# The causal mask of an attention layer: one product on the whole array, or four on parts of it

## Chip, core and metric

The kernel runs on one core of a Trainium2 chip. The metric is the device time of one execution in microseconds (us). The engines of the core run side by side, each through its own list of instructions: TensorE (matrix products; PE in the profile, its weight loads PEld), VectorE (DVE), ScalarE (ACT), GpSimd (POOL) and SyncE (SP, which issues DMAs). SBUF is the core's memory and PSUM is where TensorE writes; both have 128 partitions.

## What is computed

Two transformer layers on 4 sequences of 512 tokens of 256 features: layer 0 is causal attention with 16 heads of 16 features and a mixture of experts, layer 1 is attention and a gated network with 4-bit weights. The change is in layer 0's attention:

```python
x = x + _L0_attn_ref(_layernorm(x, axis=-1), L0_attn_w_project, L0_attn_w_out)
# in _L0_attn_ref:
qkv = jnp.einsum('bsd,od->bso', x, w_project)      # q, k, v of 16 heads
att = jnp.einsum('bhqd,bhkd->bhqk', q, k) / math.sqrt(HEAD_DIM)
causal = jnp.triu(jnp.ones((s, s), dtype=bool), k=1)
att = jnp.where(causal[None, None, :, :], jnp.float32(-1000000000.0), att)
att = jax.nn.softmax(att, axis=-1)
out = jnp.einsum('bhqk,bhkd->bhqd', att, v)
```

## The kernel before

Tokens are handled in blocks of 128. `j` (0 to 3) is the block of queries, `s` the sequence, `g` a group of four heads; the four heads of a group lie on the four quarters of the partitions, 32 each (16 features and helper rows). A batch is one `(j, s)` with 4 groups in block 0, 2 in block 1 and 1 in blocks 2 and 3. That makes 4 + 8 + 16 + 16 = 44 batches. `nk = (j + 1) * 128` is the number of keys, `nb` the number of groups of the batch.

For each batch the following steps are made:

- `greatest(n)` (line 679) computes the scores of queries by keys, one product for each head and group: 32 rows of the array, since a head has 32 partitions. The four heads go to four PSUM tiles, one bank each, from the pool `l0_sc` of five.
- `mask(n)` (line 694) adds the causal mask to the last 128 keys of each group: a product of an identity matrix `ident_h` (bf16) with `later` (bf16, 0 where the key is not later than the query, -1e30 elsewhere), added to the scores in PSUM. There is one product for each of the four heads; it repeats `later` for the `nb` groups. Then VectorE takes the largest score of each query (line 706).
- `shift(n)` (line 711) turns these maxima (line 716) and four DMAs of SP write them into a helper row of the queries (line 721).
- `powers(n)` (line 728) computes the scores a second time, keys by queries, with the maxima subtracted by the helper rows (line 738). ScalarE takes the exponential (line 747) and GpSimd clears what is later than the query (line 757).
- `mixed(n)` (line 765) multiplies by the values (line 774), on 32 columns of the array for each head, and ScalarE copies the result (line 782). `divided` (line 786) divides by the sum and projects.

The constants are made on GpSimd at the start, lines 498 to 511: a fill of `qk` with -1, a fill with 0, the copy `ident_h`, the fill and the select of `later`. Behind them on GpSimd stand the two powers of the first normalisation (line 653), then the fills of `blanks` (lines 520 to 522), the power of line 182, the fills of line 491 and `split_biases`.

What sets the order is a plan that the program works out when it is built: TensorE, VectorE, ScalarE and GpSimd take their instructions in the order in which they are written, and SP does up to batch 3; later a scheduler places SP's DMAs. In the loop over batches (line 886), `greatest(n + 1)`, `mask(n + 1)` and `shift(n + 1)` come first, then `fill` gives a budget of TensorE and VectorE costs to streams of other work, then `mixed(n - 1)` and `powers(n)`, then a second `fill`. The streams are generators that yield an engine, a cost, a gap and a condition: projections of the next block, the logits of the experts (`lg_ps`) and their results (`eo`) by `dense` (line 249), their routing on VectorE (lines 386 to 441), and the sums. So behind a mask, TensorE finds products of these streams as a rule.

```python
        for n in range(NBT):
...
                    greatest(n + 1)
...
                    mask(n + 1)
                    shift(n + 1)
...
            fill(PE=(2.0, 2.0, 1.8, 1.6)[j], DVE=2.6)
...
                    mixed(n - 1)
                powers(n)
```

Of the kernel before, what the change touches and what calls it, by code (L numbers as in the profile page):

```python
# [9 lines left out]
BF16 = mybir.dt.bfloat16  # L10
I32 = mybir.dt.int32
AF = mybir.ActivationFunctionType
ALU = mybir.AluOpType
# [3 lines left out]
P = 128  # L17
# [6 lines left out]
NEG = -1.0e30  # L24
# [8 lines left out]
def tile_transformer(  # L33
# [18 lines left out]
    nc = tc.nc  # L52
# [23 lines left out]
    ident = const.tile([P, P], F32, name="ident")  # L76
# [9 lines left out]
    mask32 = const.tile([P, 32], F32, name="mask32")  # L86
# [377 lines left out]
    with ExitStack() as l0:  # L464
        w0 = l0.enter_context(tc.tile_pool(name="w_l0", bufs=1))
# [19 lines left out]
        def blank(j, i):  # L485
# [15 lines left out]
        )  # L501
        nc.gpsimd.memset(qk[:, :, NBLK].rearrange("p g s q -> p g (s q)"), 0.0)

        ident_h = w0.tile([P, P], BF16, name="ident_h")
        nc.gpsimd.tensor_copy(ident_h, ident)
        later = w0.tile([P, P], BF16, name="later")
        nc.gpsimd.memset(later, 0.0)
        nc.gpsimd.affine_select(
            out=later, in_=later, compare_op=ALU.is_ge, fill=NEG,
            base=0, pattern=[[-1, P]], channel_multiplier=1,  # L510
        )
        bs = b1.tile([P, 2, 512], F32, tag="hi4", name="bs")
        rows = b1.tile([P, 12, P], BF16, tag="part", name="rows")
        sel = rows[:, :8]
# [161 lines left out]
        def queries(j, g):  # L676
            return qk[:, g, 4 + j % 2]

        def greatest(n):

            j, s, gs = batches[n]
            nk = (j + 1) * P
            tiles = [ps_sc.tile([P, 512], F32, tag="sc", name=f"s1_{n}_{h}") for h in range(4)]
            for b, g in enumerate(gs):
                for h in range(4):
                    r = slice(32 * h, 32 * h + 32)
                    nc.tensor.matmul(  # L687
                        tiles[h][:, b * nk : (b + 1) * nk].rearrange("p (c k) -> p c k", k=P),
                        lhsT=queries(j, g)[r, s], rhs=qk[r, g, : j + 1, s, :],
                        start=b == 0, stop=False,  # L690
                    )
            open_scores[n] = tiles

        def mask(n):

            j, s, gs = batches[n]
            nk, nb = (j + 1) * P, len(gs)
            tiles = open_scores.pop(n)
            for ps in tiles:
                nc.tensor.matmul(  # L700
                    ps[:, : nb * nk].rearrange("p (b k) -> p b k", b=nb)[:, :, j * P :],
                    lhsT=ident_h, rhs=later.unsqueeze(1).to_broadcast([P, nb, P]),
                    start=False, stop=True,
                )
            for h, ps in enumerate(tiles):
                nc.vector.tensor_reduce(  # L706
                    maxes[:, :nb, h],
                    ps[:, : nb * nk].rearrange("p (b k) -> p b k", b=nb), AX.X, ALU.max,
                )
# [126 lines left out]
        ps = ps_mm.tile([P, 4, P], F32, tag="mm", name="idle")  # L836
        for i in range(5):
            nc.tensor.matmul(
                ps, lhsT=ident, rhs=ident.unsqueeze(1).to_broadcast([P, 4, P]),
                start=not i, stop=i == 4,  # L840
# [33 lines left out]
        for piece in inputs_T(1, second[0], xT):  # L874
            pass
        greatest(0)
        mask(0)
        shift(0)
        inputs = {1: Stream(projections(1, xT))}
# [6 lines left out]
        for n in range(NBT):  # L886
            j, s, gs = batches[n]
# [7 lines left out]
            with tc.high_priority(offset=AHEAD):  # L895
                if n + 1 < NBT:
                    greatest(n + 1)
                if n + 1 < NBT:
                    mask(n + 1)
                    shift(n + 1)  # L900
# [76 lines left out]
    with ExitStack() as l1:  # L977
# [3 lines left out]
        for kv, i in [(slice(None), slice(HPK + 1, HPK + 2))] + [  # L981
            (slice(kv, kv + 1), slice(0, HPK + 1)) for kv in range(NKV)
        ]:
            for hc in range(2):
                tc.keep_in_program_order(
                    nc.sync.dma_start(
                        out=wqkv[:, hc, kv, i], in_=w_qkv[hc * P : (hc + 1) * P, kv, i]
# [239 lines left out]
        for p in range(-1, NP):  # L1227
            j, kv = divmod(p, NKV)
# [59 lines left out]
    with ExitStack() as f1:  # L1288
# [186 lines left out]
        f, k = firsts  # L1475
# [3 lines left out]
        for i in range(NBLK * NJ):  # L1479
            j, jj = divmod(i, NJ)  # L1480
# [160 lines left out]
```

## Time and profile before

| what | value |
|---|---|
| median of 3 runs | 1139.03 us (1138.77 to 1139.43) |
| profiled execution, its own time | 1140.53 us |
| its span, first to last instruction | 1138.8 us |
| granted TensorE clock, mean | 0.999 |
| ScalarE, GpSimd busy | 509.5 us (45%), 247.2 us (22%) |
| mask, line 700: loads, products | 176, 176; from 24.0 to 354.5 us |
| product of 128, 256, 512 columns: mean length | 222, 275, 382 ns (128, 32 and 16 times) |
| weight load of the mask: mean length | 97 ns |

The profile is of one execution. Lengths of products reach from the first column entering to the last result written, so that successive products overlap: the distance from start to start tells what a product costs, and its length does not. A product in f32 stands as two passes. "128\*128" is the number of rows and columns of the array that an instruction uses; "32\*128" uses a quarter of the rows, and four such products on four quarters run side by side. The chain of work that ended last is followed back from the end, from each instruction to what released it. Time on an engine counts for the end only where this chain runs through it.

### The profile page before, as it was taken

The numbers are of one execution on the slowest core, as the hardware profiler recorded it, in microseconds if no ns is written. First come the engines' busy times: TensorE is split into PE (matmuls) and PEld (weight loads), VectorE is DVE, ScalarE is ACT, GpSimd is POOL, SyncE is SP. The second block draws the span as 40 slices with busy tenths as digits, with TensorE's granted clock in tenths as the row PEclk, the third lists the DMA queues.
The fourth block names the chain that finished last, engine by engine and source line by source line (L and its number), as shares of the span: only waits on it lengthen the run. The fifth ranks groups of instructions, "written<-read, shape, count | busy, mean of one in ns | idle before, by whom it ended". The sixth has DMA issues, their size and how long they took to land.

```text
span 1138.8 us, 19760 instructions
## 1 busy us (share of the span) xinstructions
PE 1109.8 (97%) x7430; PEld 711.7 (62%) x7430; DVE 842.3 (74%) x1856; ACT 509.5 (45%) x1190; POOL 247.2 (22%) x319
## 2 busy tenths in 40 slices
PE   9999999999999999999999999999999999999998
PEld 5666555555555445555555556556787788888885
DVE  6675988999999962867873695577479877778665
ACT  1445545665556543444444353243324444444442
POOL 8322222221111000000000000000064444353433
PEclk9999999999999999999999999999999999999999
DMA  4450010000000500000000002242002002002000
GB/s 133 110 134 5 17 25 2 2 1 3 2 2 2 184 2 1 1 1 1 1 1 1 1 2 37 66 110 68 18 1 54 22 19 75 1 19 75 18 2 19
DMA packets 32287, 35.13 MB, mean 31 GB/s; under 512 B 6024, under 2 KB 23176, under 8 KB 32192
## 3 DMA queue, kind: packets, MB, share of 16 engines
q1 hardware_dynamic: 31376, 32.69, 11.0%
q10 hardware_dynamic: 816, 1.18, 0.4%
q8 instruction: 59, 0.97, 0.3%
q14 instruction: 36, 0.29, 0.1%
HBM read 23.17 MB, written 6.29 MB: 26 GB/s over the span
## 4 chain that ended last, share of the span: by engine, by line
PE 67%; DVE 23%; ACT 4%; issue 3%; POOL 1%; DMA 1%; SPq 1%; DVEq 0%; POOLq 0%; ACTq 0%
PE qk_ps L1037 10%; PE lg_ps L249 8%; PE o L1128 8%; PE eg L963 7%; PE eo L249 7%; PE gu_first L963 5%; DVE mx L706 3%; PE yx L1344 3%; PE s L738 3%; PE s L687 3%; PE av L774 2%; PE yy L1344 2%; DVE it L1420 2%; DVE th L1419 2%; PE qk_ps L555 2%
## 5 line engine op out<-in xcount | busy, mean ns | idle before, releaser
L1037 PE MATMUL qk_ps<-xT,wqkv 128*128 128x512 f32 x320 | 148.7, 599 | 3.5 <-ACT v L1023 1.7
L249 PE MATMUL lg_ps<-rw,xT 128*128 128x512 f32 x256 | 122.5, 601 | 1.6 <-ACT aT L812 0.4
L249 PE MATMUL eo<-ew,xT 128*128 128x512 f32 x256 | 121.5, 600 | 1.1 <-ACT lg L312 0.5
L706 DVE TENSOR_REDUCE mx<-s 128x1 f32<-128x384 f32 (+3 forms) x176 | 100.5, 633 | 26.8 <-PE s L700 26.8
L1128 PE MATMUL o<-wpj,oT 128*128 128x256 f32 x512 | 119.1, 382 | 0.0
L757 POOL TENSOR_SCALAR_AFFINE_SELECT pt<-pt 128x256 f32<-128x256 f32 (+2 forms) x88 | 62.5, 715 | 243.3 <-ACT pt L747 242.5
L1128 PEld LDWEIGHTS o<-wpj,oT 128*128 128x128 f32 x512 | 96.0, 190 | 27.0 <-issue 13.5
L1037 PEld LDWEIGHTS qk_ps<-xT,wqkv 128*128 128x128 f32 x320 | 59.1, 190 | 73.2 <-issue 58.4
L747 ACT ACTIVATE pt<-s 128x512 f32<-128x512 f32 (+1 forms) x176 | 84.0, 563 | 37.6 <-PE s L738 37.6
L182 POOL TENSOR_TENSOR ln_rs<-rs_v,minus_half 128x4 f32<-128x4 f32 x12 | 13.6, 1135 | 366.0 <-DVE rs_v L181 366.0
L338 ACT ACTIVATE part<-eo,c 128x256 f32<-128x256 f32 x128 | 53.6, 472 | 84.0 <-PE eo L249 72.7
L1531 ACT COPY gu_first<-eg 128x512 f32<-128x512 f32 x28 | 16.0, 570 | 134.2 <-PE eg L963 129.9
L249 PEld LDWEIGHTS eo<-ew,xT 128*128 128x128 f32 x256 | 46.2, 190 | 46.3 <-issue 38.5
L249 PEld LDWEIGHTS lg_ps<-rw,xT 128*128 128x128 f32 x256 | 46.1, 190 | 46.3 <-issue 37.5
L1322 POOL TENSOR_TENSOR it<-it 128x512 f32<-128x512 f32 x30 | 38.2, 1273 | 146.6 <-PE gu_first L963 66.9
L312 ACT COPY lg<-lg_ps 128x512 f32<-128x512 f32 x64 | 37.6, 588 | 71.8 <-PE lg_ps L249 71.8
L1041 ACT COPY qT<-qk_ps 128x512 f32<-128x512 f32 x64 | 37.5, 586 | 64.7 <-PE qk_ps L1037 64.7
L1344 PE MATMUL yx<-it,wd 128*128 128x256 f32 x240 | 66.2, 379 | 0.0
L738 PE MATMUL s<-qk 32*128 32x128 f32 x1280 | 56.6, 287 | 0.7
L687 PE MATMUL s<-qk 32*128 32x128 f32 (+3 forms) x512 | 56.7, 465 | 0.4
L438 DVE SCALAR_TENSOR_TENSOR junk<-lg,w 128x256 bf16<-128x256 f32 x128 | 54.9, 429 | 0.0
L365 DVE TENSOR_TENSOR part<-part 128x512 f32<-128x512 f32 x32 | 22.4, 700 | 43.9 <-ACT part L338 43.9
(305 smaller groups left out, 2202.5 us busy)
## 6 DMA issues: line engine op xcount, KB each, us to landing
qk<-stage SPq DMA_DIRECT2D x56, 64.0 KB
wqkv<-in_w_qkv SPq DMA_DIRECT2D x8, 320.0 KB
rw<-in_router_w SPq DMA_DIRECT2D x8, 256.0 KB
ew<-in_expert_w SPq DMA_DIRECT2D x8, 256.0 KB
qk<-mT SPq DMA_DIRECT2D x128, 0.5 KB
wpj<-in_w_proj SPq DMA_DIRECT2D x1, 2048.0 KB
dq_sgu<-in_gate_up_s SPq DMA_DIRECT2D x64, 32.0 KB
xres<-in_x SPq DMA_DIRECT2D x3, 512.0 KB
```

The lines of the kernel that those rows point to most:

```text
L249: nc.tensor.matmul(ps, lhsT=xT[:, hc, (g % 4) * P : (g % 4 + 1) * P], rhs=w[:, hc, 2 * pair : 2 * pair + 2, :].rearrange("p e o -> p (e o) ...
L338: nc.scalar.mul(part[:, e % 4], ps[:, i], c[:, e : e + 1])
L438: stt(junk, d[:, e], 0.0, w1, ALU.is_gt, ALU.mult, accum_out=c1[:, e : e + 1])
L687: nc.tensor.matmul(tiles[h][:, b * nk : (b + 1) * nk].rearrange("p (c k) -> p c k", k=P), lhsT=queries(j, g)[r, s], rhs=qk[r, g, : j + 1, ...
L706: nc.vector.tensor_reduce(maxes[:, :nb, h], ps[:, : nb * nk].rearrange("p (b k) -> p b k", b=nb), AX.X, ALU.max,)
L738: nc.tensor.matmul(tiles[h][:, at : at + P], lhsT=qk[r, g, c, s, :], rhs=queries(j, g)[r, s], start=True, stop=True,)
L747: nc.scalar.activation(pt[:, i, : nb * nk], tiles[2 * pair + i][:, : nb * nk], AF.Exp, scale=0.25)
L757: nc.gpsimd.affine_select(out=last, in_=last, compare_op=ALU.is_ge, fill=0.0, base=0, pattern=pattern, channel_multiplier=-1,)
L963: nc.tensor.matmul(ps[:, w], lhsT=lhs(w), rhs=rhs, start=start and not i and not w, stop=i == len(terms) - 1 and w == 1, skip_group_check= ...
L1037: nc.tensor.matmul(ps, lhsT=wqkv[:, hc, kv, h, :], rhs=xT[:, hc, :], start=hc == 0, stop=hc == 1,)
L1128: nc.tensor.matmul(ys[t // 2][:, t % 2], lhsT=state["o"][:, h, t * P : (t + 1) * P], rhs=wpj[:, HPK * kv + h, :], start=kv == 0 and h == 0 ...
L1344: nc.tensor.matmul(ps, lhsT=lhs(jj), rhs=its[8 * j + jj][:, plane], start=start and not n, stop=n == 1, skip_group_check=not start,)
```

## The change

The identity becomes `pick`, 32 x 32 identities on each of the four quarters of the partitions (a copy of `mask32`, which VectorE has made from `ident` by then). `later` is selected quarter by quarter, so that each quarter holds the mask of its own 32 queries against keys counted from the quarter's own first. In `mask`, each head has four products in place of one, one for each 32 queries `c`. A product takes 32 rows of the array (those of the head's quarter) and 32 columns (those of the queries), and writes only the keys from `32 * c` on: 128, 96, 64 and 32 keys per group. The order is by `c`, then by head. The scores' own products now carry the flag `stop`, and the mask products skip a check of groups when the program is built.

```diff
-        ident_h = w0.tile([P, P], BF16, name="ident_h")
-        nc.gpsimd.tensor_copy(ident_h, ident)
+        pick = w0.tile([P, 32], BF16, name="pick")
+        nc.gpsimd.tensor_copy(pick, mask32)
         later = w0.tile([P, P], BF16, name="later")
         nc.gpsimd.memset(later, 0.0)
-        nc.gpsimd.affine_select(
-            out=later, in_=later, compare_op=ALU.is_ge, fill=NEG,
-            base=0, pattern=[[-1, P]], channel_multiplier=1,
-        )
+        for i in range(4):
+            r = slice(32 * i, 32 * i + 32)
+            nc.gpsimd.affine_select(
+                out=later[r], in_=later[r],
+                compare_op=ALU.is_ge, fill=NEG, base=0, pattern=[[-1, P]], channel_multiplier=1,
+            )
...
-                        start=b == 0, stop=False,
+                        start=b == 0, stop=b == len(gs) - 1,
...
-            for ps in tiles:
-                nc.tensor.matmul(
-                    ps[:, : nb * nk].rearrange("p (b k) -> p b k", b=nb)[:, :, j * P :],
-                    lhsT=ident_h, rhs=later.unsqueeze(1).to_broadcast([P, nb, P]),
-                    start=False, stop=True,
-                )
+            for c in range(4):
+                for h, ps in enumerate(tiles):
+                    r = slice(32 * h, 32 * h + 32)
+                    left_of = P - 32 * c
+                    nc.tensor.matmul(
+                        ps[32 * c : 32 * c + 32, : nb * nk].rearrange(
+                            "p (b k) -> p b k", b=nb
+                        )[:, :, j * P + 32 * c :],
+                        lhsT=pick[r],
+                        rhs=later[r, :left_of].unsqueeze(1).to_broadcast([32, nb, left_of]),
+                        start=False, stop=True, skip_group_check=True,
+                    )
```

## The prediction

> **What bounds the kernel now.** I read the page first, for who is busy and what the chain of work that ended last is made of:
>
> ```profile
> PE 1109.8 (97%) x7430; PEld 711.7 (62%) x7430; DVE 842.3 (74%) x1856; ACT 509.5 (45%) x1190; POOL 247.2 (22%) x319
> ...
> PE 67%; DVE 23%; ACT 4%; issue 3%; POOL 1%; DMA 1%; SPq 1%; DVEq 0%; POOLq 0%; ACTq 0%
> ```
>
> The second line is the chain by engine: TensorE sets most of the end and VectorE a quarter of it, so time on TensorE counts only where the chain runs through TensorE. The mask products stand in line 700, all 176 of them between 24 and 355 us. So I read the timeline of TensorE around one batch of block j = 2:
>
> ```profile
> 150.64 0.93 PE L687 MATMUL s<-qk 32*128 32x384 f32 x8
> 151.50 0.40 PE L700 MATMUL s<-later,ident_h 128*128 128x128 bf16 x4
> 151.74 1.94 PE L249 MATMUL eo<-ew,xT 128*128 128x512 f32 x4
> 153.60 0.86 PE L774 MATMUL av<-pt,va 128*32 128x128 f32 x24
> 154.40 1.58 PE L738 MATMUL s<-qk 32*128 32x128 f32 x24
> 156.33 0.70 PE L249 MATMUL eo<-ew,xT 128*128 128x512 f32 x1 [0.35 <-DVE xres L831]
> ```
>
> Columns: start, length, line, rows*columns of the array, shape, count. The four mask products start 0.06 us apart ((0.40 - 0.219)/3, where 219 ns is the median length in the table of line 700), and 0.24 us after their start the next work is there. So the mask is cheap already: 0.24 us of a batch of 7.6 us.
>
> Two more things stand in these lines. First, a change of shape costs a pause. The mask starts 0.86 us after L687, whose products stream only 2 x 0.32 us (384 columns, two passes, and L249's 512 columns take 0.43 us a pass) behind a first load of 0.11 us: 0.11 us over. L774 streams six groups of 0.109 us from 153.60, that is until 154.28 to 154.30, and L738 starts at 154.40. The same mask followed by another shape shows it alone:
>
> ```profile
> 182.19 0.40 PE L700 MATMUL s<-later,ident_h 128*128 128x128 bf16 x4
> 182.51 0.86 PE L774 MATMUL av<-pt,va 128*32 128x128 f32 x24
> ```
>
> 0.33 us to the next work here (182.18 by the load) against 0.24 above: **94 ns for the change of shape**. Second, a load that nothing covers. L249's first product lasts 648 ns behind the mask, 697 ns behind a wait (156.33) and 592 ns otherwise: its weights cost 105 ns when they are loaded after a pause, 56 ns when they were loaded during the mask.
>
> Last, the chain in order of time, for which mask products stand on it:
>
> ```profile
> 27.56 0.97 PE s L700 x4
> ...
> 55.23 0.54 PE s L700 x4
> ...
> 122.14 0.33 PE s L700 x4
> ...
> 145.01 0.18 PE s L700
> ```
>
> "x4" means that the chain passes through the mask to the next product: 1 of 4 batches in block 0 (512 columns), 6 of 8 in block 1 (256), 13 of 32 in blocks 2 and 3 (128). A single one means that it leaves through the first mask product to VectorE's maximum: 2 times in block 0, 5 times in blocks 2 and 3. In the others VectorE is last, and the mask is covered.
>
> **The change part by part.** In the built order of the changed program each batch has 16 loads and 16 products of 32 x 32 in place of 4 and 4; everything else on TensorE, VectorE and ScalarE stands in the same order. The columns streamed are 128, 96, 64 and 32 per head and group, in place of 128.
>
> *What 16 small products take.* No row shows 32*32. The nearest is L774, also narrow in columns:
>
> ```profile
> 153.60 0.32 PE L774 MATMUL av<-pt,va 128*32 128x128 f32 x4
> ```
>
> Four of 297 ns within 0.32 us: 7 ns from start to start. The bounds: 7 ns for all 16, and 60 ns, the pitch of the present mask. I take 10 ns, near the closer row, since four tiles are shown and sixteen are not. The load of 32 columns adds 25 ns (297 against 272 in L774's table).
>
> *Blocks 2 and 3.* Before: 238 ns to the next product and 56 ns of its load uncovered, 294 ns. After: 15 x 10 ns, 25 ns load, 14 ns for 32 columns: 189; then what is new, a change of shape, since 32*32 is followed by 128*128: 94; then the load uncovered: 105. That is 388 ns, 94 more, on the chain 13 times: **+1.2 us**.
>
> *Block 1.* Before 55.17 to 55.61 in the timeline, 0.44 us, with the next load wholly covered. After 150 + 25 + 27 (64 columns) + 94 + 105 = 401 ns: about -45 ns, 6 times: **-0.3 us**.
>
> *Block 0.* Before 27.49 to 28.36, 0.88 us. After: the first four end at 30 + 25 + 213 = 268 ns, later than the last; with 199 ns behind it 467: **-0.4 us**, once.
>
> *The first maximum.* A head's scores are complete with its fourth product. The first head had that after 230 ns; now with the thirteenth of the 16, at 120 + 25 + 179 (219 less 40 for 96 columns fewer) = 324 ns: +94 ns, 5 times: **+0.5 us**. In block 0 the long first product (0.39 us) hides it.
>
> *The start.* POOL makes the constants, and this stands on the chain:
>
> ```profile
> 5.57 0.29 POOL L508 TENSOR_SCALAR_AFFINE_SELECT later<-later 128x128 bf16<-128x128 bf16 x1
> 5.84 1.52 POOL L653 TENSOR_TENSOR ln_rs<-rs_v,minus_half 128x2 f32<-128x2 f32 x2
> ...
> 20.69 0.61 POOL L533 CAST bh<-bs 96x512 bf16<-96x512 f32 x1
> ...
> 25.71 0.60 POOL L539 CAST rows<-br 32x512 bf16<-32x512 f32 x1
> ```
>
> The select becomes four on 32 partitions. L533 and L539, the same cast on 96 and on 32 partitions, show that fewer partitions take the same time (0.61, 0.60). So each of the four takes 0.27 to 0.28 us from start to start (5.57 to 5.84): 3 x 0.28 more. The copy ahead of it narrows from 128 columns (0.29 us) to 32; one of 1 column (L520) takes 0.19, so about 0.08 less. Behind them wait the two powers of L653, then VectorE's normalisation, the power of L182, POOL's first fill of L491 and SP's first store of line 568 (14.3 us): the chain passes through all of these, and the last load of the first scores lands that much later. **+0.76 us**; at worst 0.84, and 0 if the select went with the partitions.
>
> *Costed at nothing.* The changed program's SP order puts one store of L568 ahead of the four of a batch near 132 us: 0.6 us, while its reader in L738 comes 7 us later. The 528 added pairs pass through TensorE's queue, which holds work ahead (loads start 7 ns apart); if it did not, that is the third rival.
>
> Sum: 0.76 + 1.2 - 0.3 - 0.4 + 0.5 = **+1.7 us**. The profiled execution spans 1138.8 us and took 1140.53 us; spans would go to 1140.5. It ran 1.5 us above the median of 1139.03 us, so for a median I add to that: **1140.7 us**, +0.15%. (At 7 ns the sum is +0.7 us.)
>
> One rule speaks against this. The trace shows 7 ns between products on different column groups. The Trainium skill, "TensorE: Matmul & The Clock Gate", section "Wait — 56ns, not 53.3ns?", says that start-to-start never falls below about 25 ns however few the columns; its "Part 3: Packing small matmuls" gives about 4 ns between tiles of a pack. By 25 ns the sum would be +7.1 us, by 4 ns -0.2 us. L774 contradicts the 25 ns for four tiles; nothing here shows it for sixteen.
>
> **The rivals.** *Serial column groups*: the four column groups of one row quarter stream one after another, 320 columns per group in place of 128. Against it: L774's four column groups run side by side. Blocks 2 and 3: 46 + 133 + 199 = 378, +84 x 13 = 1.1; block 1: 512, +0.4; block 0: 778, -0.1; with 0.5 and 0.76: +2.6 us, **1141.6 us**.
>
> *Slow starts*: the pair of load and product is the limit. L774's 24 products take 0.86 us, less the last's 0.27: 25 ns each on average, which is their streaming but could be read as a pace. At 25 ns: blocks 2 and 3 613 ns, +4.1; first maximum +1.4; block 1 +1.1; block 0 -0.2; start 0.76: +7.1 us, **1146.1 us**. At 60 ns: 11.0 + 3.5 + 4.2 + 0.3 + 0.76, about +20 us. It decides from 12 ns a pair on, where the sum passes 2.3 us.
>
> *No pause (faster)*: 32*32 shares its row quarters with L687's 32*128 and changes shape freely, before and behind. 94 ns fall away before 27 masks on the chain (20 passed, 7 left by the first) and 94 behind 20: -4.4 us, so -2.7 us, **1136.3 us**. It decides once both pauses are missing; one alone leaves -0.8 or -0.2. Against it: every change seen costs 94 ns, also that from L249 to L774, where the rows stay 128.
>
> *Not done*: the built order shows 32 x 32 tiles at 16 different places; excluded.
>
> **How the numbers follow.** The sum 0.45, serial groups 0.20, slow starts 0.23, no pause 0.12. A measurement of this kernel tells 0.2% (2.3 us) from no change, so the sum is "same", serial groups and slow starts "slower", no pause "faster". Range: from 1137.0, which leaves out only the whole of the last rival, to 1147.0, which takes in slow starts to 25 ns and leaves out the end at 60.
>
> **What would show it.** In the profile after: a row 32*32 x704; in a batch of block 2 the 16th product some 0.15 us (0.11 to 0.38) after the first; L249 0.09 to 0.1 us behind the last column, its first product lasting 697 ns; POOL's L653 starting near 6.6 us; the first scores near 24.3 us in place of 23.6. Wrong would be: 16 products over 0.5 us or longer, L249 with no pause, or VectorE waiting for the mask in more than the 14 places of now.

## The result and the profile after

| | before | changed |
|---|---|---|
| median of 6 executions each, us | 1139.97 (1138.77 to 1141.38) | 1144.51 (1142.67 to 1144.96) |
| ratio, 95% interval | | 1.0036 [1.0023, 1.0048] |
| span of the profiled execution, us | 1138.8 | 1142.8 |
| TensorE's mean granted clock in it | 0.999 | 0.996 |

Three of before's six executions are those of the table ahead (1139.03, 1138.77, 1139.43 us); the three others took 1140.52 to 1141.38. The changed kernel is slower, by some 4 us. The time lies in the range of the prediction, but the case that was called likeliest, no measurable change, is not what came. On the page of the changed kernel the busy time by engine, the chain by engine, and the group of VectorE's maxima read:

```profile
PE 1111.3 (97%) x7958; PEld 710.3 (62%) x7958; DVE 841.7 (74%) x1856; ACT 509.1 (45%) x1190; POOL 247.1 (22%) x322
...
PE 67%; DVE 23%; ACT 3%; issue 3%; POOL 1%; DMA 1%; SPq 1%; DVEq 0%; POOLq 0%; ACTq 0%
...
L714 DVE TENSOR_REDUCE mx<-s 128x1 f32<-128x384 f32 (+3 forms) x176 | 100.5, 632 | 31.8 <-PE s L705 31.5
```

The chain has not moved to another engine. VectorE waits 31.5 us for the mask now, 26.8 before, and in 13 places, 14 before. So the page tells that something small grew, but not where 4 us come from.

The mask itself did nearly what it was meant to do. The timeline of TensorE in one batch of block j = 2 (start, length, line, rows*columns, shape, count):

```profile
153.80 0.93 PE L689 MATMUL s<-qk 32*128 32x384 f32 x8
154.66 0.23 PE L705 MATMUL s<-later,pick 32*32 32x128 bf16 x16
154.82 1.99 PE L249 MATMUL eo<-ew,xT 128*128 128x512 f32 x4
```

By the trace's single records all 16 products start within 50 ns, 3.3 ns apart, and the next work starts 0.165 us after the first; its first product lasts 697 ns, as forecast. So the surplus is elsewhere. It was found by setting the start of the same batch's mask in one trace against the other. The changed kernel is behind by 0.85 us at batch 0, 2.08 at batch 2, 1.70 at batch 8, 3.47 at batch 9, 3.00 at batch 12, 3.48 at batch 19, 3.92 at batch 43 and 4.0 at the end. Two steps stand out. The first lies in eight products of line 557 behind the second mask, here after and then before:

```profile
28.71 0.61 PE L705 MATMUL s<-later,pick 32*32 32x512 bf16 x16
29.25 4.80 PE L557 MATMUL qk_ps<-xT,wp 128*128 128x512 f32 x8
```

```profile
27.49 1.04 PE L700 MATMUL s<-later,ident_h 128*128 128x512 bf16 x4
28.36 3.60 PE L555 MATMUL qk_ps<-xT,wp 128*128 128x512 f32 x8
```

The same eight products take 1.20 us more. The second step is in four products of line 249, which have nothing to do with the change; after, then before:

```profile
92.61 3.50 PE L249 MATMUL lg_ps<-rw,xT 128*128 128x512 f32 x4 [0.24 <-ACT xT L293]
```

```profile
90.77 1.99 PE L249 MATMUL lg_ps<-rw,xT 128*128 128x512 f32 x4 [0.24 <-ACT xT L293]
```

Equal products that take longer point at the clock. The stretches of the changed kernel (start and end, length, TensorE's busy time and products, **granted clock**, DMA share, GB/s) show it:

```profile
24.67:28.08 3.41, 2.72 (x48) 1.00 0.09 32
28.08:31.49 3.41, 3.41 (x29) 0.50 0.02 2
89.52:92.93 3.41, 2.10 (x10) 1.00 0.13 20
92.93:96.34 3.41, 3.41 (x12) 0.50 0.02 5
168.03:171.44 3.41, 2.56 (x32) 1.00 0.00 0
171.44:174.85 3.41, 3.41 (x50) 0.50 0.02 5
```

Three stretches of 3.41 us ran at half clock. Before had one, and none at the first two places:

```profile
24.67:28.08 3.41, 3.18 (x37) 1.00 0.02 5
28.08:31.49 3.41, 3.41 (x11) 1.00 0.02 2
88.50:91.90 3.40, 2.63 (x11) 1.00 0.02 5
163.60:167.00 3.40, 2.77 (x17) 1.00 0.02 3
167.00:170.40 3.40, 3.40 (x35) 0.50 0.02 5
```

So the 4.0 us of these two executions are: the start +0.85; half clock at 28 us +1.2, at 93 us +1.8, and about +0.3 at 171 us, where it meets more work than before's did; block 1's masks on the chain -0.9; the first maxima of blocks 2 and 3 about +0.5. That is 3.8; 0.2 is left over.

### The profile page after: what moved, and what is told of

The parts are those of the page before. It is cut to its first block, busy times and chain, and to the rows that moved or that the text cites. A ratio compares the mean times of both kernels' runs of the same rounds, so it can differ in the third digit from the quotient of the medians.

```text
span 1142.8 us, 20824 instructions
## 1 busy us (share of the span) xinstructions
PE 1111.3 (97%) x7958; PEld 710.3 (62%) x7958; DVE 841.7 (74%) x1856; ACT 509.1 (45%) x1190; POOL 247.1 (22%) x322
## 4 chain that ended last, share of the span: by engine, by line
PE 67%; DVE 23%; ACT 3%; issue 3%; POOL 1%; DMA 1%; SPq 1%; DVEq 0%; POOLq 0%; ACTq 0%
PE qk_ps L1045 10%; PE lg_ps L249 8%; PE o L1136 8%; PE eg L971 7%; PE eo L249 7%; PE gu_first L971 5%; DVE mx L714 3%; PE yx L1352 3%; PE s L746 3%; PE s L689 2%; PE av L782 2%; PE yy L1352 2%; PE qk_ps L557 2%; DVE it L1428 2%; DVE th L1427 2%
## 5 line engine op out<-in xcount | busy, mean ns | idle before, releaser
L714 DVE TENSOR_REDUCE mx<-s 128x1 f32<-128x384 f32 (+3 forms) x176 | 100.5, 632 | 31.8 <-PE s L705 31.5
L746 PE MATMUL s<-qk 32*128 32x128 f32 x1280 | 59.0, 290 | 0.8
L746 PEld LDWEIGHTS s<-qk 32*128 32x128 f32 x1280 | 47.1, 188 | 13.6 <-issue 9.3
```

What stands on the lines that cost most here:

```text
L714: nc.vector.tensor_reduce(maxes[:, :nb, h], ps[:, : nb * nk].rearrange("p (b k) -> p b k", b=nb), AX.X, ALU.max,)
L746: nc.tensor.matmul(tiles[h][:, at : at + P], lhsT=qk[r, g, c, s, :], rhs=queries(j, g)[r, s], start=True, stop=True,)
```

## The experiments

Two theories were set at first. **A**: the half-clock stretches make most of it, and they come because the 3.41 us ahead of them use little of the array (the texts of e0 to e4 still put them down to TensorE waiting). **B**: the new mask itself makes it, as VectorE waits longer for it. Later **C** was added: a stretch is chosen by how long TensorE is busy, not by how much of the array it uses. The share used is counted here as columns streamed, times rows and columns of the tile over 128 x 128, over what 3.41 us at full clock can stream.

### The constants made later (e0_before_late, e1_after_late)

In e0 before's `ident_h` and `later`, in e1 the changed kernel's `pick` and `later`, are made behind the fills of `blanks`:

```
         nc.gpsimd.memset(qk[:, :, NBLK + 1] ...)     # last of blanks
+        nc.gpsimd.tensor_copy(pick, mask32)          # e0: ident_h, ident
+        nc.gpsimd.memset(later, 0.0)
+        nc.gpsimd.affine_select(...)                 # e1: four, e0: one
```

> The kernel before, with its mask constants (copy, fill, select: 0.8 us on GpSimd) made after the three operations of blanks, where GpSimd waits 2.4 us for VectorE. Theory A (the change's loss is GpSimd's longer start plus stretches of half TensorE clock that follow from TensorE waiting): the first scores come 0.7 to 0.8 us earlier, and the time is 0.5 to 0.8 us below the kernel before, with as many half-clock stretches (one in the profile before, at 167 us). Theory B (the loss is in the mask itself, VectorE waits longer for it): the same 0.5 to 0.8 us, and nothing else to learn. It is the base for the next three.

> The changed kernel with its constants made at that later place. Theory A: the start's 1.1 us is gone and the first scores stand as in the base; if the half-clock stretches near 28 and 93 us came from the late start alone, they go too and the time is within 0.5 us of the base; if they come from the shorter masks of blocks 0 and 1, they stay, 1.2 to 1.7 us each, and the time is 2 to 4 us above the base. Theory B: about 3 us above the base, with the half-clock stretches no more than in the base.

Measured: e0 1140.39 us, ratio 1.0001 [0.9992, 1.0010]; e1 1144.26 us, 1.0042 [1.0030, 1.0055]. The start did not get earlier, as both texts wanted it to: in e0 the first mask starts at 24.55 us, 24.04 in before. GpSimd's second power now waits 0.55 us for VectorE's `rs_v` of line 652, so that the rows behind it come only 0.1 us sooner; and the chain reaches SP's first store (line 568) through two of the fills of line 491, in before through one, so that it starts at 14.83 us in place of 14.30. So this was no way to buy the start back. But e1 and e0 have their constants in the same place, and e1 is still some 4 us behind; its stretches have

```profile
27.60:31.00 3.40, 3.40 (x29) 0.51 0.02 2
92.50:95.90 3.40, 3.40 (x4) 0.50 0.03 5
171.00:174.40 3.40, 3.40 (x52) 0.50 0.03 5
```

the same three places, with the other start. So the place of the constants is not the cause of most of it.

### Small products in half of the blocks (e3_blocks01, e4_blocks23)

From e1 and e0, whose constants are made late: the sixteen products in blocks 0 and 1 only, or in 2 and 3 only, the four whole ones elsewhere.

```
-            for c in range(4):
+            for c in range(4 if j < 2 else 0):       # e4: j > 1
...
+            for ps in () if j < 2 else tiles:        # e4: j > 1
+                nc.tensor.matmul(..., lhsT=ident_h, rhs=later..., start=False, stop=True)
...
+                if n + 1 == 12:                      # the other form of `later`
+                    nc.gpsimd.memset(later, 0.0); nc.gpsimd.affine_select(...)
```

> Base, with the 32 x 32 products in blocks 0 and 1 alone (12 batches); the constant is made anew for blocks 2 and 3. Theory A: TensorE passes these masks 0.13 to 0.45 us sooner and waits that much longer behind them; if that causes half-clock stretches, this kernel has them (clock 0.997 or less) and is 1 to 3 us above the base; without them it is 0.3 to 1 us below. Theory B: about a quarter of the loss, 1 us, since 12 of 44 batches have it, whatever the clock.

> Base, with the 32 x 32 products in blocks 2 and 3 alone (32 batches). Theory A: the next work starts 0.02 us sooner behind each of the 13 masks on the chain, so 0 to 0.4 us below the base, with the base's clock. Theory B: three quarters of the loss, 2 to 3 us above the base.

Measured: e3 1143.89 us, 1.0042 [1.0029, 1.0054]; e4 1145.00 us, 1.0048 [1.0034, 1.0061]. e3 has half clock at 27.1 and 92.0 us, where the small products of blocks 0 and 1 are, as A wants, and at 170.5 us, where its masks are whole (e0 has one there too, at 168.0 us). But half clock does not carry the whole difference, since the edit added a wait of its own, at batch 12:

```profile
125.40 0.38 PE L716 MATMUL s<-later,ident_h 128*128 128x128 bf16 x4 [1.14 <-POOL later L916]
```

By the starts of the masks in the two traces, e3 is level with e0 at batch 1 and 2.6 us behind it at the end. Batch 2 adds 0.74, batch 9 1.8, the remade constant 1.07, and the small masks take back some 0.9; from batch 13 on, with whole masks, nothing is added.

e4 met neither expectation, and the reason is again my edit. TensorE waits for the remade constant, and then the clock halves (its timeline, then two of its stretches):

```profile
125.63 0.21 PE L705 MATMUL s<-later,pick 32*32 32x128 bf16 x1 [0.91 <-POOL later L916]
126.36 0.97 PE L705 MATMUL s<-later,pick 32*32 32x128 bf16 x15 [0.52 <-POOL later L916]
```

```profile
24.40:31.10 6.70, 6.70 (x43) 0.50 0.05 15
126.70:130.10 3.40, 3.30 (x19) 0.51 0.00 0
```

From batch 11 to 13 that costs 3.7 us. The profiled execution, its slowest (1147.70 us), also had 6.7 us at half clock near the start, where its mask is that of before: that place can halve with whole masks too. What e4 does tell is the rest: from batch 15 to 43, with the small masks of blocks 2 and 3, it loses only 0.54 us against e0 (both have one half-clock stretch on the way, at 174.5 and 168.0 us). That fits the later first maxima, told below.

### Unused products (f1_after_full, f2_after_small, f3_before_full)

If A is right, more use of the array ahead of the stretches must bring full clock back. f1 adds five unused products of the identity to the changed kernel: 512 columns ahead of the scores of batch 0 and behind its mask, and 256 ahead of the transpositions that line 249's products of blocks 0, 1 and 2 wait for. f2 makes the same products, equally long, on a 32 x 32 part. f3 is f1's addition in before.

```
+        def keep_busy(cols, name):
+            ps = ps_mm.tile([P, 4, P], F32, tag="mm", name=name)
+            r = slice(0, 128)                        # f2: slice(0, 32)
+            nc.tensor.matmul(ps[r, : cols // P], lhsT=ident[r, r],
+                rhs=ident[r].unsqueeze(1).to_broadcast([128, cols // P, P]), start=True, stop=True)
...
+            if b < 3 and not hc: busy[0](256, f"busy_h{b}")
...
+        keep_busy(512, "busy0")
         greatest(0)
         mask(0)
+        keep_busy(512, "busy1")
```

> The changed kernel plus five products that compute nothing used, on the whole array (128*128, f32): 512 columns ahead of and behind the first mask, 256 columns ahead of the first transposition of each of the blocks 0, 1 and 2, where TensorE waits for VectorE anyway. Theory A (TensorE's clock falls to half for 3.4 us after a stretch of 3.4 us in which too little of the array was in use; the small masks took use away): worked out from the traces so far, weighting each streamed column by its share of the array, all nine stretches that were followed by half clock had 0.24 to 0.39 of full use and the others 0.38 or more; these products lift the stretches near 25 and 91 us above 0.4, so the half-clock stretches near 28 and 93 us go, and the time falls by 2 to 3.5 us from the changed kernel, to 1 us around the kernel before. Rival C (they come from TensorE being idle, whatever its products are): the same. Rival B (the loss lies in the mask and VectorE's wait): no change, or up to 1 us more.

> The same five products in the same places with the same columns, on 32 rows and 32 columns: the same TensorE time, a sixteenth of the array. Theory A: the half-clock stretches stay, and the time is that of the changed kernel or up to 1 us above it. Rival C: they go as with the whole array, 2 to 3.5 us below the changed kernel.

> The kernel before with the five products on the whole array. Theory A: its half-clock stretch near 167 us (0.37 of full use ahead of it) goes where the product of block 1 falls into the stretch ahead; 0.5 to 1.5 us below the kernel before, clock 0.999 or 1.000. Rival B: no change, or up to 1 us more.

Measured: f1 1140.00 us, 1.0005 [0.9996, 1.0014], 9 of 11 executions at a mean clock of 0.998 or more; the two others, at 0.995, took 1142.11 and 1142.81 us, and no trace shows where. f2 1143.17 us, 1.0023 [1.0013, 1.0033]: 9 of 11 executions at 0.994 to 0.997 (1142.7 to 1144.66 us) and two at 1.0 (1139.94 and 1140.06). f3 1139.31 us, 0.9994 [0.9985, 1.0003], all of its 11 executions within 1139.02 to 1139.68 us, while before reached 1142.66 beside it; f3's profiled execution still has a half-clock stretch, at 185.7 us, and it is the fastest, 1139.02: half clock there costs nothing. The gain of 0.5 to 1.5 us that was expected of f3 did not come in the median, as 19 of before's 33 executions beside it took 1139.2 us or less; what went is the slow part of before's spread. f1's stretches at the places shown:

```profile
24.67:28.08 3.41, 3.30 (x60) 1.00 0.08 29
28.08:31.49 3.41, 3.41 (x40) 1.00 0.01 2
89.52:92.93 3.41, 2.88 (x11) 1.00 0.02 5
92.93:96.34 3.41, 3.41 (x68) 1.00 0.01 1
```

More work makes the changed kernel some 4 us faster (3.5 by the two ratios to before), which refutes B as the main part. And f2 has the same instructions with the same lengths; the added product in f1's timeline, and in f2's:

```profile
25.38 1.12 PE L741 MATMUL busy<-ident 128*128 128x512 f32 x2
```

```profile
25.43 1.02 PE L741 MATMUL busy<-ident 32*32 32x512 f32 x2
```

It keeps TensorE as busy and does not keep the clock: C is refuted, and what counts is how much of the array the products use. f2 took away rows and columns together (32 of 128 each), so the pair does not tell whether it is the area or the rows alone. f2's profiled execution is one of its two without half clock, so the stretches of the others were not seen; their clock and time are all that shows them (one stretch of 3.41 us at half clock takes 0.0015 from the mean).

### The start alone (e2_start_only)

Before, with three more selects on 32 partitions behind the one that is there (they change nothing in `later`):

```
+            for i in range(3):
+                r = slice(32 * i, 32 * i + 32)
+                nc.gpsimd.affine_select(out=later[r], in_=later[r], compare_op=ALU.is_ge, fill=NEG,
+                    base=32 * i, pattern=[[-1, P]], channel_multiplier=1)
```

> The kernel before with GpSimd's added work alone: three further selects on 32 partitions behind the first (they change no value). The two powers behind them start 1.0 us later and the first scores come 0.8 to 0.9 us later. Theory A: the time is 0.7 to 1.0 us above the kernel before, and the clock as in it (one stretch at half clock); if the later start alone makes the stretches near 28 and 93 us, 3 to 4 us above. Rival B: 0.7 to 1.0 us.

Measured: 1140.04 us, 1.0005 [0.9996, 1.0014]. By the median alone this would say nothing, as before itself has half clock in part of its executions. Set the fast groups of executions side by side: before 1138.9 us (19 of 33), e2 1140.0 (8 of 11), so +1.1; by the starts of the masks in e2's trace it is 0.9. e2's profiled execution has no half-clock stretch, and none of its executions a mean clock under 0.999: the late start alone does not bring those of the changed kernel. GpSimd's timeline of the changed kernel and of e2:

```profile
5.48 1.35 POOL L510 TENSOR_SCALAR_AFFINE_SELECT later<-later 32x128 bf16<-32x128 bf16 x4
6.92 1.51 POOL L655 TENSOR_TENSOR ln_rs<-rs_v,minus_half 128x2 f32<-128x2 f32 x2
```

```profile
5.94 0.95 POOL L514 TENSOR_SCALAR_AFFINE_SELECT later<-later 32x128 bf16<-32x128 bf16 x3
6.97 1.52 POOL L659 TENSOR_TENSOR ln_rs<-rs_v,minus_half 128x2 f32<-128x2 f32 x2
```

A select on 32 partitions takes 0.33 to 0.37 us from its start to the next one's, and the power starts 1.1 us late in both. With f1 (1139.8 us without half clock) and f2's two (1139.94, 1140.06) this parts the change: they are 0.9 to 1.1 us above before's 1138.9, of which the unused products are 0.2 to 0.4 (most of f3's executions took 1139.1 to 1139.3). So the change costs 0.5 to 0.9 us without half clock; the start is 0.9 to 1.1 of it, and **the new mask with its maxima is worth between nothing and -0.6 us**, an estimate from these differences.

### The order of the sixteen (h1_heads_first)

f1 with the two loops exchanged, so that a head's four products follow each other:

```
-            for c in range(4):
-                for h, ps in enumerate(tiles):
+            for h, ps in enumerate(tiles):
+                for c in range(4):
```

> The changed kernel with the five whole-array products, and the 16 mask products ordered by head and then by quarter of the queries, in place of the other way. In the changed kernel VectorE's first maximum, where it waits, starts 361 ns after the mask (267 before), although the first head's last product starts 42 ns after it. If the lag is the thirteenth place of that product, the first maximum comes 30 to 40 ns sooner; if it is the signal that waits for the whole pack of 16, nothing moves; if the four products of a row quarter stream one after another when they are issued together, the next work comes later than 165 ns after the mask's start. Time within 0.5 us of the changed kernel with the five products.

Measured: 1139.55 us, 0.9998 [0.9989, 1.0006], against f1's 1140.00 with 1.0005 [0.9996, 1.0014]: no certain difference in the medians; the fastest executions are 0.5 us apart (1139.23 and 1139.72). The trace is plainer. The same mask and the maximum behind it, after and then h1:

```profile
179.12 0.23 PE L705 MATMUL s<-later,pick 32*32 32x128 bf16 x16
...
179.48 1.95 DVE L714 TENSOR_REDUCE mx<-s 128x1 f32<-128x384 f32 x4 [2.44 <-PE s L705]
```

```profile
174.33 0.26 PE L708 MATMUL s<-later,pick 32*32 32x128 bf16 x16
...
174.62 1.95 DVE L717 TENSOR_REDUCE mx<-s 128x1 f32<-128x384 f32 x4 [0.82 <-PE s L708]
```

VectorE starts 361 ns behind the mask's start by the changed order, 286 by this one, 267 in before: 75 ns sooner, where 30 to 40 or nothing was expected. The next work on TensorE comes at 195 ns in place of 165. That is not a row quarter's products in turn: by the records the last head's first product, 128 columns or 53 ns, starts at 40 ns, and 102 ns lie behind its last column, as behind the changed order's last product (50 ns, 13 ns for 32 columns, 102).

### A version that beats both (b1_best)

The gains kept, the costs left: small products in blocks 0 and 1 only, the four whole ones in 2 and 3, the five unused products, and one constant made by one select (224 columns hold the shifted triangles of all four row quarters). The identity is read as the upper halves of the float32 one, so its copy goes away.

```
-        ident_h = w0.tile([P, P], BF16, name="ident_h"); nc.gpsimd.tensor_copy(ident_h, ident)
+        ident_h = ident.bitcast(BF16).rearrange("p (q two) -> p q two", two=2)[:, :, 1]
-        later = w0.tile([P, P], BF16, name="later")
+        later = w0.tile([P, 224], BF16, name="later")     # select with pattern [[-1, 224]]
...
+            for c in range(4 if j < 2 else 0):            # lhsT=ident_h[r, r],
+                ...                                       # rhs=later[r, 32 * h : 32 * h + left_of]
+            for ps in () if j < 2 else tiles: ...         # as before, rhs=later[:, :P]
```

> A version meant to beat both: the small products in blocks 0 and 1 alone, the whole product in blocks 2 and 3, both from one select over 224 columns (a quarter reads it from its own column on) and from ident itself read as bf16, so that GpSimd makes no copy; and the five whole-array products. Theory A: the start loses about 0.2 us, blocks 0 and 1 about 0.9 us, and the clock stays full: 0.7 to 1.1 us below the kernel before's undisturbed 1138.9 us, and no runs at half clock, so 1138.0 us (0.1%). If the small masks bring half clock in spite of the five products, 1139 to 1142.

Measured: 1138.61 us (1138.16 to 1140.13, 11 executions) against 1140.58 for before on the same chip, ratio 0.9987 [0.9978, 0.9996]. Its profiled execution spans 1136.4 us at a clock of 1.0. It beats before by 0.13% and the changed kernel by about 0.5%, the two ratios taken together. Part of that is only that before sometimes halves its clock: the fastest executions of the two there, 1138.16 and 1138.83 us, are 0.7 us apart. No execution at half clock was expected; three of its 11 took 1140.04 to 1140.13 us at a mean clock of 0.999, which looks like one such stretch, and no trace shows it.

## Why the prediction was right or wrong

The time lay in the range, but not for a reason that the prediction named: the range reached so high for slow starts of the products, and they are fast. That it held is luck. **The step that failed is the one that isn't there**: the sum was made of durations at full clock, and took the clock for given, though before's own trace holds a half-clock stretch at 167.0 us. Without half clock the change costs 0.5 to 0.9 us, inside the forecast "same"; of the 4.0 us between the two profiled executions 3.3 are half clock (1.2, 1.8 and 0.3).

What comes ahead of a half-clock stretch could be read from twelve traces, by the share of the array used in the 3.41 us before it. Take 24.67 to 28.08 us. In the changed kernel the quarter-array products of line 689 there use 0.78 us of full array and the small masks 0.13: 0.91 of 3.41, 0.27. In before the whole-array mask alone is worth 0.81 us, and with line 687's 0.85 the share is 0.49 in the same time. f1 adds two passes of 512 columns on the whole array (0.85 us) and has 0.54, f2's on 32 x 32 parts count 0.05 and leave 0.31. The fifteen stretches of full clock that were followed by half clock had 0.25 to 0.38. Of the other stretches up to 400 us (some 1350, their limits counted on from the clock's first rise in each trace), all had 0.38 or more but three: 0.34 at 87.6 us in f2, 0.35 at 44.4 us in h1 and 0.36 at 43.2 us in b1. The share of time in which columns stream does not sort them: in f3 0.78 was followed by half clock, and 0.39 to 0.41 in h1, b1, e0 and others was not.

Area is not the only count that fits. If a product counts by its rows alone, whatever its columns, the fifteen had 0.31 to 0.40 and the others 0.395 or more, with one of them out of order in place of three. Against rows alone stand f2's times: by this count half or more of the possible positions of its stretches would leave full clock at both of the first places, and 2 of 11 executions had it. How rows and columns share in it stays open; no run changed one without the other.

The change made four whole-array products into sixteen on a sixteenth each, so that it took from the array's use exactly where the kernel is thin. Around the first masks, which are four groups wide, it is the products' own size. Ahead of batch 9 it is in part a wait: the stretch from 89.52 us holds no mask, only whole-array products, but the mask ahead of it is over sooner (the next product starts 0.21 us after the mask, 0.45 in before), and TensorE then waits 0.54 us for VectorE's `xn` in place of 0.22. In most of blocks 2 and 3 the full-array products of line 249 beside the mask keep the share up.

In each trace the clock changes only at whole multiples of 3.413 us from its first rise (it falls after 47 of them in before, after 6 in the changed kernel). The stretches do not come in every execution, since this raster lies differently each time. Over the possible positions of the raster, windows with an area share below 0.385 take up 0.16 (20 to 34 us), 0.02 (84 to 100) and 0.74 (160 to 178) of them in before, and 1.17, 1.05 and 0.80 in the changed kernel (over 1: a position can hold two). By this estimate, what happened now and then, mostly in one place, now happens nearly always in two and often in the third. That the raster is free is inferred from the differing places; no run set it.

The Trainium skill, "TensorE: Matmul & The Clock Gate", section "Part 1: The HAM clock gate (the "warmup" mystery)", has a gate of half or full clock, ruled by a free-running window of 3413 ns. The traces agree with the length (3.41 us) and the halves (0.50). The page sees the danger in idle time, of about that length or in frequent short gaps; here TensorE stood idle for only 0.7 to 1.3 us of the windows ahead of the three stretches, and f1 against f2 shows that how much of the array the products use counts too.

By its own terms:

- **Pitch of the small products**: 10 ns taken, 3.3 ns measured. "Slow starts" (25 ns and more) is refuted, and with it the case for which the upper end of the range stood.
- **Pause and load**: 94 ns taken, 102 measured behind 32*32 products (165 ns less 50 of starts and 13 of columns); the load of 105 ns was uncovered as said. "No pause" is refuted. "Serial column groups" too: in block 1 the next load comes at 217 ns, which is the longest product's 107, 10 for its start, and 100.
- **Blocks 2 and 3**: +94 ns per mask on the chain forecast; 270 ns against 291 measured (235 and 56 for the load), -21. **Block 1**: -45 forecast, 322 against 447 ns, -125. **Block 0**: 428 against 875, -0.45 us, about as forecast. The common fault is the pitch, and a guessed 25 ns that the starts already held.
- **First maximum**: +94 ns forecast and measured, but for the wrong reason. The first head's last product starts 40 ns behind the mask's first, not 120; what came on top is a late signal, told below.
- **Start**: +0.76 forecast; the power starts 1.08 us late. Four selects on 32 partitions take 1.44 us from the first's start to the power's, 0.36 each and not 0.28: the term was mis-sized because two casts stood for a select.

With the measured terms and the forecast's counts the masks come to -1.5 us (-21 x 13, -125 x 6, -450 ns) in place of +0.5, the maxima to +0.5 and the start to +1.1: +0.1 us. The 0.5 to 0.9 found without half clock is 0.4 to 0.8 more. Where that went stays open; the counts are those of before's chain, and a mask that ends sooner can leave VectorE last. (The prediction's own terms add up to 1.76 us, where it writes 1.7, and to -0.3 at 4 ns, where it writes -0.2.)

## What to carry to other kernels

In this kernel the part of the array that a product uses was not only a cost. Before making products smaller, count the array's use over each 3.4 us around them, and look for half-clock stretches in the trace at hand. Where the use is thin, an unused whole-array product in a gap can pay for itself. And price a constant's preparation by the instruction's own row: here four selects on a quarter of the partitions took 1.44 us and the one on all of them 0.27.

## What the runs showed that was not expected

- **Half clock follows the use of the array, not only its idle time.** Equally long unused products on 128 x 128 gave 1140.00 us, on 32 x 32 1143.17.
- **Select on GpSimd**, at the start of the kernel: 0.29 us for 128 x 128, 0.28 to 0.30 for 32 x 128, 0.37 for 128 x 224. The fewer partitions bought nothing. The selects of e3 and e4 near 125 us took up to 0.66 us in either shape.
- **Signals of packed products come late.** In the changed kernel the first head's signal comes 114 ns behind the recorded end of that head's last product (15 ns in before), and the later heads' 34 ns apart, the last 206 ns behind the end of the pack. With the head's products first in the pack the first signal is earlier by 74 ns (h1), and the last comes at the same time, 441 ns behind the mask's start. The Trainium skill, "TensorE: Matmul & The Clock Gate", section "The cost: per-tile semaphore tail", gives 25 + 4.7 x 16 + 26.3 = 126 ns behind a pack of 16 with one signal, and 26.3 ns for each more, so 205 ns with four; the last signal's 206 ns agrees. When the earlier ones come, which h1 changes, isn't in its formula.
- **The start of 16 products on 16 tiles takes 50 ns**, and products that share a row quarter don't run one after the other: in the changed order those of the first head start at 0, 13, 26 and 40 ns, and the first of them streams for 53.
